# A graph layer on one core: VectorE builds the cells' matrix, its product and the two larger node comparisons in halves

## The chip, the cores and the metric

One core of a Trainium2 chip runs the kernel. The metric is the device time of one execution in microseconds; of several executions the median is taken. Five engines work from queues of their own, each in order: TensorE (PE: matmuls, with the weight loads listed apart as PEld), VectorE (DVE), ScalarE (ACT), GpSimd (POOL, which issues the gathers here) and SyncE (SP, which issues the other transfers). [...]

## The reference

The reference is one layer of a graph network with a residual and a normalization. There are 12,500 nodes with 128 features and 400,000 edges, sorted by their destination. Each edge carries the row of its source through one of two matrices, chosen by its type, and the results are summed per destination:

```python
Xs = X[src]
m_data = Xs @ W_data.T + b_data
m_ctrl = Xs @ W_control.T + b_control
msg = jnp.where((edge_types == 0)[:, None], m_data, m_ctrl)
agg = jax.ops.segment_sum(msg, dst, num_segments=X.shape[0])
out = relu(agg + (X @ W_self.T + b_self))
x = _layernorm(x + out)
```

## The kernel before

The sum over the edges comes first, by type, and the matrices are applied to the sums; so the heavy part is a gather of 400,000 rows and a sum by destination. The edges are 3,125 chunks of 128, in 25 groups of 125 chunks. A group has five windows, and a window five chunks of one kind and twenty of the other.

The five chunks are gathered by GpSimd: an indirect DMA (`fetch`, L828) fetches 128 rows into `msg`. VectorE makes a 0/1 matrix `psel` that says to which destination column each edge goes (`choose` in `gathered`, L850, by `select`, L533), and TensorE multiplies (`add_rows`, L755).

The twenty chunks, 2,560 edges, take another way that needs no gather. There are 107 of these windows, and in the text a window is one of them. The whole node table `x3` stands in SBUF as 98 blocks of 128 rows, and the edges are sorted on the chip by the block of their source into 100 cells of 32 slots. For window `w` this happens in the steps of `give_slots`:

- `block_matrix` (L592): VectorE compares each edge's block number with the 100 cell numbers and writes the 0/1 matrix `O`, 128 x (20 x 100).
- `fours` (L608): sums of chunks of `O` into `prod` (L612, L613). `same_lane` (L597): which chunks of one lane share a block (L602).
- `before` (L615): TensorE counts the edges ahead in the same cell (L622) into PSUM.
- `ranks` (L627): VectorE adds the two counts into `ahead` (L630), multiplies `O` by it into `prod` (L634), and sums `prod` along each row in three steps (L639 twice, L641) into `found`; `rank` is its copy (L643).
- `rank_matrix` (L670): VectorE makes `rm` (L533) and `rv` (L674) from the rank. `put` (L681): TensorE multiplies `O` and `rv` (L686), which puts each edge's lane and code into its cell.
- `spread`, `turn_codes`, `keep_codes`: the cells go through DRAM to all partitions (`pick`) and the codes into `code`.
- In every second window `over` finds edges beyond slot 32 (`key`, `top`, `full`, `over_n`, `bits`), and `spare_slots` gives them 64 spare slots by `om_all` (L558), which TensorE reads at L562.
- `pick_matrix` (L736): VectorE turns `pick` into a 0/1 matrix in place (L741).

Then `picked` (L910) sums the window: TensorE picks the rows of 25 cell quadruples from `x3` (L930, into `got`), ScalarE copies them to `emsg` (L944), VectorE compares each slot's code with the destination columns into `esel` (`choose` in `picked`, L919: 10 quadruples at once, then 9, then 6, each 176 columns wide), and TensorE sums them (L755) into `sums`. VectorE adds `sums` to `acc` and the counts to `cnt` (L817). `sums` has two PSUM banks, the pool of `esel` two buffers, `prod` one.

`finish_batch` multiplies the sums by the weights, and normalizes and writes the rows.

Steps of several windows run beside each other. The program names each step with a place in its window (numbers between 0 and 1), `merged` sorts them, and the framework's scheduler then fixes the order on each engine by dependencies; so the order on VectorE is not quite that of the source. No order is written out by hand, but `issue_after` and `paced` hold some steps behind others.

Of the kernel before, what the change touches and what calls it, by code (L numbers as in the profile page):

```python
# [9 lines left out]
BF = mybir.dt.bfloat16  # L10
# [4 lines left out]
OP = mybir.AluOpType  # L15
# [4 lines left out]
P = 128  # L20
# [9 lines left out]
EC = 20  # L30
# [7 lines left out]
EW = 88  # L38
# [8 lines left out]
NCELL = 4 * NQ  # L47
# [159 lines left out]
def short_path(ctx, tc, const, ident, eps, wT, brow, bad, x, src, dst, etype, ws, bs, out):  # L207
    nc = tc.nc
# [126 lines left out]
    def table(n, base, name):  # L335

        t = keep.tile([P, n], BF, name=name)
        nc.vector.tensor_copy(t, iota([n], [[1, n]], base, 0, f"{name}_i"))
        return t

    cell_cols = [keep.tile([P, NCELL], BF, name=f"cell_col{k}") for k in range(2)]
# [6 lines left out]
    code_col = table(2 * EW, 1, "code_col")  # L348
# [177 lines left out]
    slots, placed = {}, []  # L526
    pairs = len(each_e)

    def select(sel, col, code2):

        rows, n, width = sel.shape
        shape = [rows, n, width // 2, 2]
        nc.vector.tensor_tensor(  # L533
            sel.rearrange("p n (w t) -> p n w t", t=2),
            col[:rows].rearrange("p (o w t) -> p o w t", o=1, t=2).to_broadcast(shape),
            code2.rearrange("p n (o t) -> p n o t", o=1).to_broadcast(shape),
            op=OP.is_equal,
        )
        return sel

    joint = {}

    def spare_slots(w, at):
# [39 lines left out]
    def give_slots(w):  # L583
        g, i = each_e[w]
        blk = codes["e", g][0][:, i]
        blk2, vals2, pk = (t[:, i * CHUNKS + PB:(i + 1) * CHUNKS] for t in codes["e", g][1:])
        s = {}
# [4 lines left out]
        def block_matrix():  # L592
            O = s["held"] = two.tile([P, EC * NCELL], BF, name="O")
            s["O"] = O.rearrange("p (c j) -> p c j", j=NCELL)
            select(s["O"], cell_cols[w % 2], blk2)

        def same_lane():  # L597
            eq = s["prod"][:, :, NCELL:]
# [28 lines left out]
        def ranks():  # L627
            ahead = two.tile([P, NCELL], BF, name="ahead")
            with nc.allow_low_precision(reason="whole numbers; those over 256 need not be exact"):
                nc.vector.tensor_reduce(  # L630
                    ahead, s["ahead"][:, :2 * NCELL].rearrange("p (k j) -> p j k", k=2), AX.X, OP.add
                )
            prod = s["prod"]
            nc.vector.tensor_tensor(  # L634
                prod[:, :, :NCELL], s["O"], ahead.rearrange("p (o j) -> p o j", o=1).to_broadcast([P, EC, NCELL]),
                op=OP.mult,
            )
            for h in ((NCELL + EC) // 2, (NCELL + EC) // 4):
                nc.vector.tensor_add(prod[:, :, :h], prod[:, :, :h], prod[:, :, h:2 * h])  # L639
            found = two.tile([P, EC], FP, name="found")  # L640
            nc.vector.tensor_reduce(found, prod[:, :, :h], AX.X, OP.add)  # L641
            rank = s["rank"] = two.tile([P, EC, 2], BF, name="rank")
            nc.vector.tensor_copy(rank, found.rearrange("p (c o) -> p c o", o=1).to_broadcast([P, EC, 2]))  # L643
# [103 lines left out]
    def sums():  # L747
        return ps2.tile([P, 512], FP, name="sums")

    def cells_of(ps, width, k):  # L750
        return ps[:, k * 2 * width:(k + 1) * 2 * width]

    def add_rows(out, msg, sel, start, stop):
        for j in range(3):
            last = nc.tensor.matmul(  # L755
                out, msg[:, j * D:(j + 1) * D], sel, start=(start and j == 0), stop=stop, skip_group_check=True
            )
        return last
# [54 lines left out]
    def accumulate(at, rows, ps, wide, width):  # L813

        n = rows.shape[1]
        win = rows[:, :, bass.ds(at, width)]
        added.append(nc.vector.tensor_add(win, win, ps[:, :n * wide].rearrange("p (a w) -> p a w", w=wide)[:, :, :width]))  # L817
# [15 lines left out]
    def paced(now, gate):  # L833

        if spare:
            gather = spare.pop()()
        elif to_fetch and due[len(due) - len(to_fetch)] <= now:
            gather = fetch()
        else:
            return  # L840
        tc.add_manual_dep(
            gather.ins, gate.ins.name,
            mybir.DependencyInfo(mybir.DependencyClass.Sync, mybir.DependencyReason.DATA), reason="paced",
        )
# [65 lines left out]
    def picked(w, tiled, ending, before):  # L910

        g, i = each_e[w]
        s = {"sel": {}, "msg": {}}
        bounds = [0, 5, 10, 15, 19, NQ - 1]
        turns = len(bounds) - 1

        def choose(q0, n):  # L919

            sel = select(sp.tile([P, 10, 2 * EW], BF, name="esel")[:, :n], code_col, slots[w]["code"][:, q0:q0 + n])
            for k in range(n):
                s["sel"][q0 + k] = sel[:, k]

        lead = 0 if w % 2 else 2
        half_rows = slice(CAP * lead, CAP * lead + OVF)

        def pick(ps, q, a0=0, a1=4):
            for a in range(a0, a1):
                last = nc.tensor.matmul(  # L930
                    ps[CAP * a:CAP * (a + 1), :], slots[w]["pick"][:, a * NQ + q, :],
                    x3[:, 4 * q + a - a0].rearrange("p j d -> p (j d)"), start=True, stop=True, skip_group_check=True,
                )
            return last

        def rows(q, n, room, half=False):
            ps = psg.tile([P, room, 512], FP, name=f"got{room}")
            msg = two.tile([P, room, 3 * D], BF, name=f"emsg{room}")
            for k in range(n):
                last = pick(ps[:, k, :3 * D], q + k)  # L940
                s["msg"][q + k] = msg[:, k, :]
            if half:
                last = pick(ps[:, n, :3 * D], NQ - 1, lead, lead + 2)
            s["out"] = nc.scalar.copy(msg[:, :n], ps[:, :n, :3 * D])  # L944
            if half:
                nc.scalar.copy(s["msg"][NQ - 1][half_rows, :], ps[half_rows, n, :3 * D])
            return last

        def add(q0, q1):
            done = [  # L950
                add_rows(cells_of(s["ps"], EW, 0), s["msg"].pop(q), s["sel"][q], q == 0, q == NQ - 1)
                for q in range(q0, q1)
            ]
            return done[len(done) // 2 - 1], done[-1]

        def unit(t):

            if t == 3:
                assert not spare
                if "both" in slots[w]:  # L960
                    slots[w]["last"] = two.tile([P, 3 * D], BF, name="last", bufs=1)
                s["msg"][NQ - 1] = slots[w]["last"]
            paced(w + (t + 0.5) / turns, rows(bounds[t], 2, 2))
            if t == 1 and w > 0 and w % 2 == 0:
                spare.append(lambda: spare_rows(w))
            gate = rows(bounds[t] + 2, bounds[t + 1] - bounds[t] - 2, 3, t == 3)
            if t == 0:
                choose(0, 10)
                gates = ending() or [gate]
            if t == 1:  # L970
                choose(10, 9)
            if t == 3:
                choose(19, NQ - 19)
            while counts:
                c = counts.pop(0)
                count(c["ps"], c["sel"])
            if t == 1:
                s["ps"] = sums()
            if t == 1 and before:
                before()  # L980
            if t > 0:
                gates = add(bounds[t - 1], bounds[t])
            paced(w + (t + 1) / turns, gates[0])
            if t == 2:
                paced(w + (t + 1) / turns, gates[-1])
            for u in tiled.get(t, []):
                u()
            if t == 0 and w + 1 < pairs and "own_turn" in slots[w + 1] and w > 0:
                slots[w + 1]["own_turn"]()
            if t == turns - 1 and "both" in slots[w]:  # L990
                with tc.issue_after(s["out"].ins):
                    nc.scalar.copy(slots[w]["last"][:OVF, :], slots[w]["both"][:OVF, :])

        def end():

            early, *more = tiled.get(turns, [lambda: None])
            early()
            gates = add(bounds[turns - 1], NQ)
            for u in more:
                u()  # L1000
            accumulate(place_of(g, 2 * i + 1), acc_rows(g, 0, 2), s["ps"], EW, EW)
            return gates

        return evenly([lambda t=t: unit(t) for t in range(turns)]), end
# [138 lines left out]
    sp = ctx.enter_context(tc.tile_pool(name="sel", bufs=2))  # L1143
# [13 lines left out]
    n = 0  # L1157
# [11 lines left out]
    def ending():  # L1169
        pass  # L1170
# [191 lines left out]
```

## Time and profile before

| what | value |
|---|---|
| median of 3 runs | 1741.98 us (1740.0 to 1743.36) |
| the profiled execution | 1746.84 us, its span 1745.0 us |
| VectorE instructions in the profile | 3677 |
| granted TensorE clock, mean | 0.993 |

The profile is of one execution. A row of the groups gives line, engine, operation, tiles and shapes, the count, then busy us and mean ns of one, then the idle time of the engine just before them and what ended it. A row of the waits says which engine stood, at what, for whom, with the total in us, the count and the longest. The chain of waits is followed back from the last instruction. A mean over forms hides that L533 serves six uses: `O`, `psel`, `rm`, and `esel` in three widths.

### The profile page before, as it was taken

The page shows a single profiled execution, that of the slowest core. Times are in us where ns is not written, and L with a number is a line of the kernel's source. Part 1 is how long each engine was busy: PE and PEld are TensorE (multiplying, and loading weights), DVE is VectorE, ACT ScalarE, POOL GpSimd, SP SyncE. Part 2 cuts the span into 40 slices and gives each one's busy share as a digit, 9 for nine tenths or more (in the row PEclk, how much of TensorE's full clock was granted, in tenths as well). Part 3 has the DMA queues.
Part 4 walks back from the last instruction along what each step waited for, and adds up shares of the span by engine and source line. Part 5 has one row for each costly group of instructions (what it writes and reads, how often), then busy time and mean ns, then how long its engine had stood idle before and what let it go on. Part 6 is the DMA issues. An engine that isn't in the chain of part 4 may idle for free.

```text
span 1745.0 us, 67260 instructions
## 1 busy us (share of the span) xinstructions
PE 1588.9 (91%) x28154; PEld 1238.1 (71%) x28154; DVE 1555.4 (89%) x3677; ACT 1249.5 (72%) x2251; POOL 1266.2 (73%) x1061
## 2 busy tenths in 40 slices
PE   0599999999999999999999999999999999999997
PEld 0377777777777777777777777777777777777776
DVE  7898899999899899899998898999998898998983
ACT  5777777777777777767777777776777676777675
POOL 0277777887778777777777677787777788768772
PEclk9999999999999999999999999999999999999999
DMA  7844454544454444444545444545454545444431
GB/s 202 276 125 145 129 151 129 156 145 145 126 156 127 143 150 139 137 137 131 155 124 160 133 145 129 153 127 155 135 156 127 150 125 146 143 146 126 128 123 59
DMA packets 148966, 248.22 MB, mean 142 GB/s; under 512 B 35937, under 2 KB 115260, under 8 KB 148652
## 3 DMA queue, kind: packets, MB, share of 16 engines
q1 hardware_dynamic: 85994, 134.45, 23.4%
q0 software_dynamic: 50032, 102.98, 22.0%
q10 hardware_dynamic: 12626, 6.40, 1.4%
q8 instruction: 222, 3.64, 0.8%
q14 instruction: 92, 0.75, 0.1%
HBM read 226.24 MB, written 17.50 MB: 140 GB/s over the span
## 4 chain that ended last, share of the span: by engine, by line
PE 43%; DVE 41%; issue 8%; ACT 4%; DMA 3%; DVEq 0%; SPq 0%; POOL 0%; ACTq 0%; POOLq 0%
PE sums L755 19%; PE got L930 14%; DVE esel L533 5%; DVE prod L639 4%; PE side L1049 4%; DVE pick L741 4%; DVE rv L674 3%; DVE found L641 3%; DVE prod L634 3%; DVE prod L612 2%; DVE psel L533 2%; ACT emsg L944 2%; DVE rm L533 2%; PE side L622 2%; DVE O L533 1%
## 5 line engine op out<-in xcount | busy, mean ns | idle before, releaser
L828 POOL DMA_INDIRECT msg<-rows,idx_g x985 | 1194.3, 1213 | 349.0 <-issue 134.4
L944 ACT CAST emsg<-got 128x768 bf16<-128x768 f32 (+1 forms) x1070 | 953.4, 930 | 340.9 <-PE got L930 325.0
L755 PE MATMUL sums<-esel,emsg 128*128 128x176 bf16 x7704 | 693.6, 240 | 2.2 <-DVE acc L817 1.9
L755 PEld LDWEIGHTS <-emsg 128*128 128x128 bf16 x7704 | 566.8, 98 | 111.6 <-issue 104.2
L930 PE MATMUL got<-x,pick 128*32 128x384 bf16 x10486 | 591.9, 331 | 17.8 <-DVE pick L741 10.6
L930 PEld LDWEIGHTS <-pick 128*32 128x32 bf16 x10486 | 242.0, 96 | 139.5 <-DVE pick L741 13.8
L533 DVE TENSOR_TENSOR esel<-code_col,code 128x1760 bf16<-128x1760 bf16 x321 | 293.2, 913 | 20.4 <-PE sums L755 19.0
L755 PE MATMUL sums<-psel,msg 128*128 128x48 bf16 x2955 | 184.3, 184 | 39.8 <-DVE cnt L817 35.8
L755 PEld LDWEIGHTS <-msg 128*128 128x128 bf16 x2955 | 152.6, 97 | 72.9 <-issue 69.4
L639 DVE TENSOR_TENSOR prod<-prod 128x1200 bf16<-128x1200 bf16 x214 | 133.7, 625 | 4.7
L634 DVE TENSOR_TENSOR prod<-O,ahead 128x2000 bf16<-128x2000 bf16 x107 | 128.3, 1199 | 2.7
L533 DVE TENSOR_TENSOR O<-cell_col,blk 128x2000 bf16<-128x2000 bf16 x107 | 127.3, 1189 | 0.5 <-ACT blk L437 0.5
L817 DVE TENSOR_TENSOR acc<-acc,sums 128x176 f32 (+2 forms) x232 | 66.5, 289 | 58.2 <-PE sums L755 49.2
L741 DVE TENSOR_SCALAR pick<-pick,lane_f 128x3200 bf16<-128x3200 bf16 x107 | 112.8, 1054 | 2.8 <-DMA pick<-there 2.8
L905 POOL DMA_INDIRECT both<-rows,idx x54 | 66.5, 1231 | 61.8 <-ACT emsg L944 43.1
L686 PE MATMUL side<-rv,O 128*128 128x64 bf16 x2140 | 84.5, 195 | 21.1 <-DVE rv L674 20.0
L533 DVE TENSOR_TENSOR psel<-near_col,near 128x1200 bf16<-128x1200 bf16 x125 | 96.1, 769 | 0.0
L686 PEld LDWEIGHTS <-O 128*128 128x128 bf16 x2140 | 79.7, 100 | 23.0 <-DVE rv L674 19.8
L674 DVE TENSOR_TENSOR rv<-rm,vals 128x1280 bf16<-128x1280 bf16 x107 | 87.8, 821 | 0.0
L641 DVE TENSOR_REDUCE found<-prod 128x20 f32<-128x600 bf16 x107 | 83.0, 775 | 2.7
L612 DVE TENSOR_TENSOR prod<-O 128x1000 bf16<-128x1000 bf16 x107 | 71.9, 672 | 0.0
L630 DVE TENSOR_REDUCE ahead<-side 128x100 bf16<-128x200 f32 x107 | 38.8, 363 | 32.8 <-PE side L622 29.5
(192 smaller groups left out, 1571.8 us busy)
## 6 DMA issues: line engine op xcount, KB each, us to landing
pick<-there SPq DMA_DIRECT2D x106, 800.0 KB
msg<-rows,idx_g POOLq DMA_INDIRECT x985
acc<-acc_start SPq DMA_DIRECT2D x23, 640.0 KB
rows<-x SPq DMA_DIRECT2D x6, 1344.0 KB
xs<-in_x_dram SPq DMA_DIRECT2D x99, 62.5 KB
out_dram<-h SPq DMA_DIRECT2D x99, 62.5 KB
xt<-in_x_dram ACTq DMA_DIRECT2D x6, 896.0 KB
cnt<-cnt_start SPq DMA_DIRECT2D x22, 160.0 KB
```

What stands on the lines that cost most here:

```text
L533: nc.vector.tensor_tensor(sel.rearrange("p n (w t) -> p n w t", t=2), col[:rows].rearrange("p (o w t) -> p o w t", o=1, t=2).to_broadcast( ...
L612: nc.vector.tensor_add(h[:, :2 * CQ], s["O"][:, :2 * CQ], s["O"][:, 2 * CQ:])
L634: nc.vector.tensor_tensor(prod[:, :, :NCELL], s["O"], ahead.rearrange("p (o j) -> p o j", o=1).to_broadcast([P, EC, NCELL]), op=OP.mult,)
L639: nc.vector.tensor_add(prod[:, :, :h], prod[:, :, :h], prod[:, :, h:2 * h])
L641: nc.vector.tensor_reduce(found, prod[:, :, :h], AX.X, OP.add)
L674: placed[:] = [nc.vector.tensor_tensor(rv.rearrange("p c v (r t) -> p c v r t", t=2), rm.rearrange("p c (o r t) -> p c o r t", o=1, t=2).t ...
L686: nc.tensor.matmul(s["rk"][:m, :2 * CAP], s["held"][:, c * NCELL:c * NCELL + m], s["rv"][:, c].rearrange("p v r -> p (v r)"), start=(c == ...
L741: nc.vector.tensor_scalar(t, t, lane_f, None, op0=OP.is_equal)
L755: last = nc.tensor.matmul(out, msg[:, j * D:(j + 1) * D], sel, start=(start and j == 0), stop=stop, skip_group_check=True)
L828: return nc.gpsimd.indirect_dma_start(out=msg, out_offset=None, in_=rows3[:, :], in_offset=bass.IndirectOffsetOnAxis(ap=codes["p", g][0][: ...
L930: last = nc.tensor.matmul(ps[CAP * a:CAP * (a + 1), :], slots[w]["pick"][:, a * NQ + q, :], x3[:, 4 * q + a - a0].rearrange("p j d -> p (j ...
L944: s["out"] = nc.scalar.copy(msg[:, :n], ps[:, :n, :3 * D])
```

## The change

Three places that issue one VectorE instruction issue two, over the first and the last half of the chunks or quadruples. `halves(n)` gives the two slices; for an odd number the first is longer (9 becomes 5 and 4). The comparison of six quadruples, `psel`, `rm` and everything else stay whole. What is computed is the same, into the same tiles.

```diff
+    def halves(n):
+        return slice(0, n - n // 2), slice(n - n // 2, n)
...
         def block_matrix():
             O = s["held"] = two.tile([P, EC * NCELL], BF, name="O")
             s["O"] = O.rearrange("p (c j) -> p c j", j=NCELL)
-            select(s["O"], cell_cols[w % 2], blk2)
+            for c in halves(EC):
+                select(s["O"][:, c], cell_cols[w % 2], blk2[:, c])
...
             prod = s["prod"]
-            nc.vector.tensor_tensor(
-                prod[:, :, :NCELL], s["O"], ahead.rearrange("p (o j) -> p o j", o=1).to_broadcast([P, EC, NCELL]),
-                op=OP.mult,
-            )
+            for c in halves(EC):
+                nc.vector.tensor_tensor(
+                    prod[:, c, :NCELL], s["O"][:, c],
+                    ahead.rearrange("p (o j) -> p o j", o=1).to_broadcast([P, c.stop - c.start, NCELL]), op=OP.mult,
+                )
...
         def choose(q0, n):
-            sel = select(sp.tile([P, 10, 2 * EW], BF, name="esel")[:, :n], code_col, slots[w]["code"][:, q0:q0 + n])
+            sel = sp.tile([P, 10, 2 * EW], BF, name="esel")[:, :n]
+            for c in halves(n) if n > 6 else [slice(0, n)]:
+                select(sel[:, c], code_col, slots[w]["code"][:, q0 + c.start:q0 + c.stop])
```

## The prediction

> **What bounds the kernel now.** I read the page first: busy times, then the chain of work that ended last.
>
> ```profile
> span 1745.0 us, 67260 instructions
> ...
> PE 1588.9 (91%) x28154; PEld 1238.1 (71%) x28154; DVE 1555.4 (89%) x3677; ACT 1249.5 (72%) x2251; POOL 1266.2 (73%) x1061
> ...
> PE 43%; DVE 41%; issue 8%; ACT 4%; DMA 3%; DVEq 0%; SPq 0%; POOL 0%; ACTq 0%; POOLq 0%
> PE sums L755 19%; PE got L930 14%; DVE esel L533 5%; DVE prod L639 4%; PE side L1049 4%; DVE pick L741 4%; DVE rv L674 3%; DVE found L641 3%; DVE prod L634 3%; DVE prod L612 2%; DVE psel L533 2%; ACT emsg L944 2%; DVE rm L533 2%; PE side L622 2%; DVE O L533 1%
> ```
>
> Two engines carry the end in turn: TensorE with 43% of the chain and VectorE with 41%. The other three are far behind. The busy time of one stretch in the steady part says how much room each of the two has:
>
> ```profile
> core 0: us, PE busy (x) PEld busy (x) DVE busy (x) ACT busy (x) POOL busy (x), PEclk, DMA share, GB/s
> ...
> 800.00:1200.00 400.00, 378.22 (x6752) 295.01 (x6749) 366.62 (x854) 289.08 (x532) 300.44 (x253) 1.00 0.47 140
> ```
>
> TensorE is idle for 22 us in 400 (5%), VectorE for 33 us (8%), and the granted clock is full. Each window (there are 107, so about 16.3 us apiece) leaves 0.9 us of idle TensorE and 1.4 us of idle VectorE. Next, the list of waits tells which of the two waits for the other, and where:
>
> ```profile
> engine line waited for: us in total, times, longest us
> ...
> DVE acc L817 <- PE sums L755: 49.2, 62, 3.4
> ...
> PE sums L755 <- DVE cnt L817: 35.8, 46, 1.9
> ...
> DVE ahead L630 <- PE side L622: 29.5, 51, 3.4
> ...
> DVE esel L533 <- PE sums L755: 19.0, 30, 1.4
> ...
> PE got L930 <- DVE pick L741: 10.6, 15, 2.7
> ...
> PE side L562 <- DVE om_all L558: 9.4, 17, 1.6
> ...
> PE sums L755 <- DVE acc L817: 3.5, 8, 1.7
> ```
>
> Both directions are there. VectorE stands for sums of TensorE (49.2 + 29.5 + 19.0 us), TensorE stands for small VectorE instructions that come late (35.8 + 10.6 + 9.4 + 3.5 us). So the kernel is a coupled pair, each nearly full, and neither more VectorE work nor an earlier small VectorE instruction is free.
>
> **The price of one more VectorE instruction.** The groups by form give the durations of what is cut:
>
> ```profile
> L634 DVE TENSOR_TENSOR prod<-O,ahead 128x2000 bf16<-128x2000 bf16 x107 | 128.3, 1199 | 2.7
> L533 DVE TENSOR_TENSOR O<-cell_col,blk 128x2000 bf16<-128x2000 bf16 x107 | 127.3, 1189 | 0.5 <-ACT blk L437 0.5
> L533 DVE TENSOR_TENSOR esel<-code_col,code 128x1760 bf16<-128x1760 bf16 x107 | 113.4, 1060 | 3.0 <-PE sums L755 2.6
> ...
> L533 DVE TENSOR_TENSOR esel<-code_col,code 128x1584 bf16<-128x1584 bf16 x107 | 104.4, 976 | 0.0
> ...
> L612 DVE TENSOR_TENSOR prod<-O 128x1000 bf16<-128x1000 bf16 x107 | 71.9, 672 | 0.0
> ```
>
> Each of four forms runs 107 times, and the change adds one instruction to each: 4 x 107 = **428** more. By durations, two instructions of 1000 elements take 2 x 672 = 1344 ns against 1189 ns for one of 2000, so 155 ns more. But durations overlap, which the order of time shows by its starts (first column, in us; the second is the duration):
>
> ```profile
> 807.04 0.67 DVE L612 TENSOR_TENSOR prod<-O 128x1000 bf16<-128x1000 bf16 x1
> 807.63 0.37 DVE L602 TENSOR_TENSOR prod<-blk,blk 128x400 bf16<-128x400 bf16 x1
> ...
> 809.30 1.06 DVE L533 TENSOR_TENSOR esel<-code_col,code 128x1760 bf16<-128x1760 bf16 x1
> 810.28 0.17 DVE L651 MAX8 top<-key 128x8 f32<-128x20 f32 x1
> ...
> 814.47 0.97 DVE L533 TENSOR_TENSOR esel<-code_col,code 128x1584 bf16<-128x1584 bf16 x1
> 815.36 1.19 DVE L533 TENSOR_TENSOR O<-cell_col,blk 128x2000 bf16<-128x2000 bf16 x1
> 816.47 0.36 DVE L630 TENSOR_REDUCE ahead<-side 128x100 bf16<-128x200 f32 x1
> ```
>
> An instruction that waits for nothing starts about 0.08 us before the one ahead of it ends. So what the queue feels is start to start: 1.11 us for 2000 elements (815.36 to 816.47), 0.59 us for 1000 (807.04 to 807.63). Two halves take 1.18 us: **0.07 us more**. The comparisons have the same rate: 0.98 us for 1760 and 0.89 us for 1584, that is 0.09 us for 176 elements or 0.51 ns each, which leaves 0.98 - 0.90 = 0.08 us fixed. I take 0.07 us for all four, since the halves wait for nothing of each other (in the built order the second half carries no wait). That is 0.28 us for a window and 428 x 0.07 = **30 us** in all, which is 2% of VectorE's busy time.
>
> [...]
>
> **What of the 30 us shows.** From below: added time shows at least where the halved instructions lie on the chain, as long as the order stays. esel has 5% of 1745 us = 87 us, at 0.83 us a piece (0.98, 0.89 and, for the uncut form of 1056 by the same rate, 0.62) about 105 pieces, of which two forms of three are cut: 70. prod L634 has 3% = 52 us, about 47 pieces of 1.11 us; O has 1% = 17 us, about 15. Together 132 pieces x 0.07 = **9 us**. From above: all 30 us, if VectorE became the only clock. Between: off the chain, VectorE's stalls for TensorE (98 us, 0.9 us a window) take the rest in windows that have such a stall. 62 + 51 + 30 stalls in 107 windows are not spread evenly, so some of the remaining 21 us shows too. I take **15 us**, nearer to the chain's count than to the full sum.
>
> **What the halves could give back.** First, an earlier start for the consumer. TensorE needs only the first columns of esel to begin. But nothing on TensorE waits for esel now; the idle time before everything that writes or reads it ends so:
>
> ```profile
> its engine sat idle before it (us, times) until:
>   PE sums L755: 19.0, 30
>   ACT last L992: 4.8, 1
>   DVE acc L817: 1.9, 2
>   PE side L504: 0.7, 1
>   ACT emsg L944: 0.2, 1
> ```
>
> No row names a VectorE esel, so this gain is nothing. O's readers (the product by ltri behind the fours, and L686) come much later, and the product with ahead goes whole into the add at L639, which waits for the second half. Nothing there either.
>
> Second, **overtaking**. VectorE takes its queue in order, and the order is not that of the source: a scheduler sets it, and with halves it can put a small instruction between them. The built order shows that it does. In 52 of 107 windows something stands between the halves of O, in 80 of 214 cases between those of a comparison, never between those of the product. Against before, about 30 instructions om_all (15 windows) stand ahead of at least half of O; about 20 adds into cnt and 44 into acc stand one half earlier; 16 reductions ahead (L630) stand earlier against O. The rest is all but unchanged: the same instructions on every engine, the order on GpSimd the same in all but two places, and no DMA added or moved past a queue that matters. What an overtaking is worth can be seen in one place:
>
> ```profile
> 465.45 1.07 DVE L533 TENSOR_TENSOR esel<-code_col,code 128x1760 bf16<-128x1760 bf16 x1
> ...
> 466.44 1.19 DVE L533 TENSOR_TENSOR O<-cell_col,blk 128x2000 bf16<-128x2000 bf16 x1
> ...
> 467.55 0.80 DVE L558 TENSOR_SCALAR om_all<-slot_col,side 128x448 bf16<-128x448 bf16 x2
> ...
> 468.41 0.34 PE L562 MATMUL side<-bits_b,om_all 128*128 128x6 bf16 x7 [0.74 <-DVE om_all L558]
> ```
>
> om_all stands behind O (1.11 us), and TensorE idles 0.74 us for it. With om_all behind half of O it would come 0.52 us earlier. The gain at a wait is thus about 0.45 us (half of 1.11, less 0.07 or so for the extra start). How often?
>
> ```profile
> L558 DVE TENSOR_SCALAR om_all<-slot_col,side 128x448 bf16<-128x448 bf16 x107 | 42.9, 439 | 5.5 <-PE side L552 3.8 <-PE sums L755 0.6 <-ACT emsg L944 0.2
> ...
> L817 DVE TENSOR_TENSOR cnt<-cnt,sums 64x120 f32 x120 | 31.6, 263 | 12.4 <-issue 5.6 <-PE sums L755 4.4 <-PE got L930 2.4
> ```
>
> TensorE waits for om_all 17 times in about 53 windows that have it; of the 15 moved ones between 5 (the average share) and 15 (all) hit a wait: 2 to 7 us, I take 4. It waits for 46 of 120 adds into cnt; 38% of 20 moved ones is 8: 8 x 0.45 = 3.5 us, at most 9. The adds into acc hold TensorE 8 times in all: 1 us. The reductions ahead pull the string ahead, L634, L639, found, rank, rm, rv forward; the chain runs through L634 in 47 of 107 windows, so 7 of 16 count, but ahead itself waits for TensorE in half of the windows: 7 x 0.5 x 0.5 = 2 us, at most 8. Sum **10 us**; bounds 0 (every overtaker only waits in front of the queue instead of behind it, as ahead and acc often do) and 25.
>
> **Sum.** 15 - 10 = **+5 us** on the profiled execution of 1746.84 us (span 1745.0, 1.8 us around it). That execution lies 4.9 us above the median of the runs shown, 1741.98 (1740.0 to 1743.36), so I put the difference on the median: **1747.0 us**. Outer bounds: 9 - 25 = -16 (1726) and +30 (1772).
>
> **Rivals.**
> - *The cost shows in full* (VectorE becomes the clock). For it: VectorE has 92% busy in the steady stretch, and the dependent string from ahead to pick holds TensorE at pick. Against it: 98 us of stalls for TensorE. It gives +18 to +30, 1760 to 1772.
> - *The stalls take it all.* For it: three of four cuts lie between pick and the next ahead, where VectorE's stalls for sums and side lie. Against: the 132 pieces on the chain. With 9 to 12 us shown and about 10 given back: 1738.5 to 1745.5, no change that can be told.
> - *Faster: overtaking outweighs the starts.* One mechanism: om_all and cnt come from behind the halves, and TensorE's 35.8 + 9.4 us of waits for them shrink. It decides from the point where more than about 9 / 0.45 = 20 waits are shortened by half an instruction while no more than the chain's 132 pieces pay. With 40 of the 63 waits shortened (40 x 0.45 = 18 us) and 9 us paid it gives -9, 1733. Against: 14 or so waits are hit by the counts above, and most waits for cnt stand behind pick and rv, which are not cut.
> - *Nothing is cut in effect* is no case: the built order has the 428 instructions.
>
> **How the numbers follow.** A measurement of this kernel can tell about 0.2% from no change, that is 3.5 us. Forecast (slower by a little, 1745.5 to 1760): 0.43. Full cost: 0.10. Stalls take it: 0.16. Faster (below 1738.5): 0.31. So slower 0.53, within 0.2% 0.16, faster 0.31. The forecast's own range is 1745.5 to 1760; for 8 in 10 it has to reach well into the faster case and into the lower part of the full cost: 1731 to 1764.
>
> **What would show it.** Right: O, esel and prod in pairs of about 0.67 and 0.6 us, start to start 0.07 us more for a pair; VectorE busy up by 20 to 30 us; the waits of TensorE for om_all down by some us, for cnt a little; the waits of VectorE for sums and side down by more than those of TensorE. Wrong: if pairs cost under 0.03 us more, if TensorE's waits for cnt and om_all fall by over 15 us (faster), or if its waits for pick and cnt rise by over 10 us (full cost). The shape of the scheduler's order over all 107 windows is what I know least: small moves of TensorE's own order could be worth as much as either sum.

## The result and the profile after

The changed kernel takes 1745.7 us (median of 20 runs, 1742.1 to 1750.01), the kernel before 1741.37 us (20 runs, 1737.15 to 1745.67). The ratio is 1.0027, 95% interval 1.0019 to 1.0035: **slower by 0.27%**, 4.7 us by the ratio. The forecast was 5 us on a median of 1741.98 us, that is 1747.0 us; its case, slower by a little, went from 1745.5 to 1760. The measured median lies 0.2 us inside that, right beside the rival in which VectorE's stalls take the starts. The time alone does not tell the two apart; the runs below have to. The two executions that were profiled happen to stand the other way round (1744.97 us after, 1746.84 us before), within the scatter of single runs; so spans of two profiles are compared below only where the difference is much larger. VectorE's busy times are compared: the durations of its 4105 instructions sum to 1859.6 us in the changed kernel and to 1860.8 us with the same halves in the order of before, 0.06% apart.

The page of the changed kernel, its span, busy times and chain:

```profile
span 1743.2 us, 67687 instructions
...
PE 1586.8 (91%) x28154; PEld 1234.6 (71%) x28154; DVE 1576.9 (90%) x4105; ACT 1249.6 (72%) x2251; POOL 1244.5 (71%) x1061
...
DVE 50%; PE 36%; issue 6%; ACT 5%; DMA 2%; DVEq 1%; SPq 0%; ACTq 0%; POOL 0%; POOLq 0%
PE sums L761 16%; PE got L938 12%; DVE esel L533 6%; DVE prod L645 4%; DVE prod L640 4%; DVE pick L747 4%; DVE rv L680 4%; DVE found L647 3%; PE side L1057 3%; DVE prod L617 3%; DVE O L533 2%; DVE psel L533 2%; ACT emsg L952 2%; DVE rm L533 2%; PE side L627 2%
```

VectorE has the 428 instructions more (4105 against 3677) and 21.5 us more of busy time (1576.9 less 1555.4). Its share of the chain goes from 41% to 50%. (L numbers behind the first cut are 5 to 8 higher than those of before. In the runs below with a held order they are up to 49 higher, most of it for the code that holds the order.) The halves by form:

```profile
L533 DVE TENSOR_TENSOR esel<-code_col,code 128x880 bf16<-128x880 bf16 x321 | 188.8, 604 | 4.0 <-PE sums L761 3.6
L533 DVE TENSOR_TENSOR O<-cell_col,blk 128x1000 bf16<-128x1000 bf16 x214 | 138.7, 668 | 0.5 <-ACT blk L437 0.5
L640 DVE TENSOR_TENSOR prod<-O,ahead 128x1000 bf16<-128x1000 bf16 x214 | 135.9, 676 | 2.3
...
L533 DVE TENSOR_TENSOR esel<-code_col,code 128x704 bf16<-128x704 bf16 x107 | 55.4, 518 | 0.0
```

And the waits that answer to those of before:

```profile
DVE acc L823 <- PE sums L761: 40.9, 56, 1.8
PE sums L761 <- DVE cnt L823: 38.7, 57, 1.8
DVE esel L533 <- PE sums L761: 21.5, 24, 1.9
DVE ahead L635 <- PE side L627: 21.0, 40, 2.2
...
PE got L938 <- DVE pick L747: 10.5, 19, 2.6
...
PE side L566 <- DVE om_all L562: 8.4, 14, 1.3
...
PE sums L761 <- DVE acc L823: 4.6, 9, 1.9
```

VectorE stands less for TensorE (40.9 + 21.0 + 21.5 = 83 us where it was 98). TensorE stands for VectorE about as long as before (38.7 + 10.5 + 8.4 + 4.6 = 62 us against 59). The prediction had expected its waits for om_all to fall by some us and those for cnt by a little; against before the first fall by 1.0 us (9.4, then 8.4) and the second rise by 2.9 (35.8, then 38.7). In this comparison nothing of the overtaking can be seen; it takes a kernel that has the starts and not the overtaking.

### The profile page after: what moved, and what is told of

Its sections match the earlier page's. It is cut to its first block, busy times and chain, and to the rows that moved or that the text cites. A ratio compares the mean times of both kernels' runs of the same rounds, so it can differ in the third digit from the quotient of the medians.

```text
span 1743.2 us, 67687 instructions
## 1 busy us (share of the span) xinstructions
PE 1586.8 (91%) x28154; PEld 1234.6 (71%) x28154; DVE 1576.9 (90%) x4105; ACT 1249.6 (72%) x2251; POOL 1244.5 (71%) x1061
## 4 chain that ended last, share of the span: by engine, by line
DVE 50%; PE 36%; issue 6%; ACT 5%; DMA 2%; DVEq 1%; SPq 0%; ACTq 0%; POOL 0%; POOLq 0%
PE sums L761 16%; PE got L938 12%; DVE esel L533 6%; DVE prod L645 4%; DVE prod L640 4%; DVE pick L747 4%; DVE rv L680 4%; DVE found L647 3%; PE side L1057 3%; DVE prod L617 3%; DVE O L533 2%; DVE psel L533 2%; ACT emsg L952 2%; DVE rm L533 2%; PE side L627 2%
## 5 line engine op out<-in xcount | busy, mean ns | idle before, releaser
L834 POOL DMA_INDIRECT msg<-rows,idx_g x985 | 1169.9, 1188 | 361.1 <-issue 121.3
L938 PE MATMUL got<-x,pick 128*32 128x384 bf16 x10486 | 590.6, 331 | 16.1 <-DVE pick L747 10.5
L533 DVE TENSOR_TENSOR esel<-code_col,code 128x880 bf16<-128x880 bf16 (+2 forms) x535 | 313.7, 607 | 23.0 <-PE sums L761 21.5
L761 PE MATMUL sums<-psel,msg 128*128 128x48 bf16 x2955 | 183.2, 184 | 44.5 <-DVE cnt L823 38.7
L533 DVE TENSOR_TENSOR O<-cell_col,blk 128x1000 bf16<-128x1000 bf16 x214 | 138.7, 668 | 0.5 <-ACT blk L437 0.5
L640 DVE TENSOR_TENSOR prod<-O,ahead 128x1000 bf16<-128x1000 bf16 x214 | 135.9, 676 | 2.3
L747 DVE TENSOR_SCALAR pick<-pick,lane_f 128x3200 bf16<-128x3200 bf16 x107 | 113.2, 1057 | 0.8 <-DMA pick<-there 0.8
L823 DVE TENSOR_TENSOR acc<-acc,sums 128x176 f32 (+2 forms) x232 | 66.5, 289 | 48.9 <-PE sums L761 40.9
L627 PEld LDWEIGHTS <-ltri 128*128 128x128 bf16 x1284 | 41.1, 96 | 36.6 <-issue 34.1
```

Source lines behind the costliest of these rows:

```text
L533: nc.vector.tensor_tensor(sel.rearrange("p n (w t) -> p n w t", t=2), col[:rows].rearrange("p (o w t) -> p o w t", o=1, t=2).to_broadcast( ...
L640: nc.vector.tensor_tensor(prod[:, c, :NCELL], s["O"][:, c], ahead.rearrange("p (o j) -> p o j", o=1).to_broadcast([P, c.stop - c.start, NC ...
L747: nc.vector.tensor_scalar(t, t, lane_f, None, op0=OP.is_equal)
L761: last = nc.tensor.matmul(out, msg[:, j * D:(j + 1) * D], sel, start=(start and j == 0), stop=stop, skip_group_check=True)
L834: return nc.gpsimd.indirect_dma_start(out=msg, out_offset=None, in_=rows3[:, :], in_offset=bass.IndirectOffsetOnAxis(ap=codes["p", g][0][: ...
L938: last = nc.tensor.matmul(ps[CAP * a:CAP * (a + 1), :], slots[w]["pick"][:, a * NQ + q, :], x3[:, 4 * q + a - a0].rearrange("p j d -> p (j ...
```

## The experiments

The theory on record: 428 extra starts of 0.07 us show in part (15 us), and small instructions that overtake half of a cut one give back part of that (10 us). Rivals: VectorE's stalls absorb the starts and overtaking is worth nothing; or the starts are free and the new order is what is slower. The two terms come apart if the order is held. Two tools did it: order-only edges (no wait) between each engine's instructions in a given order, and a second half that stands right behind its first ("glued"). The core of it, where `parts[at]` is a whole instruction, or a first half with what is glued to it, and `steps` leads through an engine's instructions in the order that is held:

```diff
+        for d in steps:
+            at += d
+            for i in parts[at]:
+                if before is not None:
+                    tc.add_manual_dep(
+                        i, before.name,
+                        mybir.DependencyInfo(mybir.DependencyClass.NoSync, mybir.DependencyReason.DATA), reason="in_order",
+                    )
+                before = i
```

In the traces, with the pieces of a cut instruction counted as one, VectorE's instructions stand in exactly the order that each run was given. VectorE has 273 semaphore instructions and 2652 instructions with a wait in before, and the same in the two runs with halves and quarters glued in its order: holding the order added no wait. The two orders differ at 768 of 3677 places on VectorE (first halves), 3006 of 27,841 on TensorE, 219 of 2233 on ScalarE and 2 of 1057 on GpSimd. So "all but unchanged", as the prediction had it for the rest of the order, holds for GpSimd alone.

All runs had five rounds beside the kernel before on the same chip: 12 executions for a cut by itself, 4 to 8 for the held orders of the whole change. Microseconds are the ratio's excess times 1741.

| kernel | median us | ratio (95% interval) | us |
|---|---|---|---|
| the change | 1745.70 | 1.0027 (1.0019 to 1.0035) | +4.7 |
| halves glued, order of before | 1754.52 | 1.0078 (1.0063 to 1.0093) | +13.6 |
| quarters glued, order of before | 1790.44 | 1.0286 (1.0269 to 1.0303) | +49.8 |
| whole, order of after, at the second half's place | 1746.49 | 1.0033 (1.0022 to 1.0044) | +5.7 |
| whole, order of after, at the first half's place | 1752.60 | 1.0067 (1.0053 to 1.0082) | +11.7 |
| halves glued, order of after | 1766.44 | 1.0142 (1.0122 to 1.0161) | +24.7 |
| halves glued, VectorE in the order of before, others of after | 1780.86 | 1.0229 (1.0212 to 1.0246) | +39.9 |
| only the cells' matrix cut | 1739.19 | 0.9982 (0.9971 to 0.9994) | -3.1 |
| only the product cut | 1743.70 | 1.0008 (0.9995 to 1.0022) | +1.4 |
| only the comparisons cut | 1745.23 | 1.0021 (1.0011 to 1.0031) | +3.7 |
| cells' matrix cut and glued, order of before | 1745.70 | 1.0027 (1.0014 to 1.0040) | +4.7 |
| cells' matrix whole, order of the run with it cut | 1741.98 | 1.0009 (0.9996 to 1.0022) | +1.6 |
| cells' matrix in quarters | 1742.17 | 0.9999 (0.9987 to 1.0011) | -0.2 |

### The starts alone

> The changed kernel with every engine held in the order of the kernel before; the second half of each cut instruction stands right behind its first half, so nothing overtakes. What is left of the change is the 428 extra starts. My theory (starts that show, less an overtaking that gives back): +9 to +15 us over before, up to 30, VectorE busy up by 20 to 30 us. Rival 'the stalls absorb the starts and the overtaking is worth nothing': +4 us, as the whole change. Rival 'the starts are free, the new order is what is slower': 0, within 2 us.

Measured: +13.6 us (11 to 16). VectorE's busy time is 28.9 us above before, 67.5 ns for each of the 428:

```profile
span 1756.4 us, 67688 instructions
...
PE 1591.8 (91%) x28154; PEld 1240.5 (71%) x28154; DVE 1584.3 (90%) x4105; ACT 1249.0 (71%) x2251; POOL 1238.0 (70%) x1061
```

Both rivals fall: the starts alone cost three times what the whole change costs, so they are neither absorbed nor free. Quarters ask what is left of the cover that VectorE's stalls give:

```diff
-        return slice(0, n - n // 2), slice(n - n // 2, n)
+        ends = [0, *(n - n * k // 4 for k in (3, 2, 1)), n]
+        return [slice(a, b) for a, b in zip(ends, ends[1:])]
```

> As the first run, but in quarters: 1284 extra starts, none overtaken, in the order of before. By 0.07 us apiece 90 us more of VectorE work, 0.84 us for a window, nearly all of VectorE's stalls of 0.9 us. My theory (the cover is used up): 35 to 60 us over before, more than three times the run with halves. Rival 'the stalls absorb the starts': under 20 us.

Measured: +49.8 us, 3.7 times the halves for three times the starts. The page and two of its waits:

```profile
PE 1595.9 (89%) x28154; PEld 1242.6 (69%) x28154; DVE 1641.5 (92%) x4961; ACT 1250.2 (70%) x2251; POOL 1242.2 (69%) x1061
```

```profile
PE sums L802 <- DVE cnt L864: 57.0, 80, 2.2
DVE acc L864 <- PE sums L802: 30.6, 45, 1.5
```

VectorE has 86.1 us more than before for 1284 starts, 67.1 ns each. Of the first 28.9 us 47% showed, of 86.1 us 58%. The waits fit that: VectorE's stalls for TensorE at acc shrink (49.2, then 30.6 us), and TensorE's for the adds into cnt grow (35.8, then 57.0 us).

### The order alone

> The kernel before, every instruction whole, with every engine held in the order of the changed kernel; a whole instruction stands where its second half stood, so the small instructions that overtook half of it now overtake all of it. No extra start. My theory: 5 to 10 us faster than before. Rival 'the stalls absorb the starts': 0, within 2 us. Rival 'the new order is slower': +4 us.

> As the run before, but a whole instruction stands where its first half stood, so the small instructions that came between the halves stand behind all of it, nearly as in the kernel before. My theory: about as before, -2 to +2 us, since the overtaking is gone and no start is added. Rival 'the new order is slower, by TensorE's own order or something else than the halves': +4 us here too.

Measured: +5.7 and +11.7 us. Both of my numbers were wrong, and the first run came near what the rival "the new order is slower" had said (+4). Without any extra start, the order of the changed kernel is slower than that of before, by 12 us where a whole instruction stands in front of what overtook its second half, and by 6 us where all of it is overtaken. So the order is not a thing that is good or bad by itself: the scheduler made it for halves, and the next two runs ask what it needs of them. The place of the small instructions is worth 6 us here (11.7 less 5.7), in the direction that I had expected.

> The changed kernel with every engine held in its own order, but the second half of each cut instruction stands right behind the first, so that the small instructions which stood between the halves stand behind both. If the give-back (9 us between halves in the order of before and the changed kernel) comes from what stands between halves: +10 to +14 us over before, like the halves in the order of before. If it comes from the rest of the new order (whole moves, TensorE's and ScalarE's orders): +4 to +6 us, like the changed kernel.

> Halves glued, VectorE in the order of before, all other engines in the order of the changed kernel. If the give-back lies in VectorE's own order: +12 to +16 us. If it lies in the order of the others: +4 to +6 us.

Measured: +24.7 and +39.9 us, both above both of their expectations. Gluing the halves in the otherwise unchanged order costs 20 us against the changed kernel, so what stands **between** halves is what that order lives on; with nothing between them it is worse than the order of before (13.6). The starts have nearly the same price in both orders: 24.7 less 11.7 is 13.0 us, where in the order of before it was 13.6. In the last run VectorE has one order and the other engines another: it takes 26 us more than the glued halves in the order of before throughout, and 15 us more than those in the order of after throughout. The orders of the engines fit each other, and that is worth at least as much as either term that was forecast (15 and 10 us).

The waits of the glued run, to be held against those of the changed kernel above:

```profile
DVE acc L863 <- PE sums L801: 44.7, 59, 1.8
PE sums L801 <- DVE cnt L863: 44.1, 60, 1.9
DVE ahead L673 <- PE side L665: 29.5, 47, 2.0
DVE esel L569 <- PE sums L801: 25.8, 28, 1.9
PE side L604 <- DVE om_all L600: 14.5, 22, 1.9
```

With the halves apart TensorE waits 6.1 us less for om_all (14.5, then 8.4) and 5.4 us less for cnt (44.1, then 38.7), and VectorE 8.5 us less for ahead.

### Each cut by itself

Two of the three loops were put back to one instruction, and the scheduler was free:

```diff
-            for c in halves(EC):
+            for c in [slice(0, EC)]:
```

> Only the comparison that makes the cells' matrix is cut, 107 extra starts (7 us of VectorE work), the scheduler free as in the change. My theory: starts show +3 us, the overtaking over it gives back 3 to 5 us, so -2 to +1 us against before. Rival 'each cut costs its share': +1 us for a quarter of the extra starts, and nothing between halves matters.

> Only the product with the counts ahead is cut, 107 extra starts, the scheduler free. Nothing ever stands between these halves, so my theory gives the starts alone, and they lie in the string that leads to pick: +3 to +6 us. Rival 'each cut costs its share of the whole': +1 us.

> Only the two larger comparisons of node columns are cut: 214 extra starts, 14 us of VectorE work, the scheduler free. If the three cuts add up: the change's +4 us less -3 (cells' matrix alone) less +1.5 (product alone) leaves +6 us. My theory agrees: starts that show 6 to 7 us (14 us at the share of the halves in the order of before), with little given back. Rival 'the gain of the cells' matrix was chance, each cut costs its share': +2 us.

Measured: -3.1 us (interval -5 to -1), +1.4 us (-1 to +4) and +3.7 us (2 to 5). They add up to +2 us, and the change has +4.7 (3 to 6): the same within the intervals. The comparisons came out between my +6 and the rival's +2. The product is cheaper than I had said and near the rival's +1; its VectorE busy time is 4.3 us up where 107 starts make 7.2. Nothing stands between its halves in any of the 107 windows, so nothing overtook a half of it: the scheduler moved other instructions. **The cells' matrix alone beats both kernels**, by a little more than I had expected; it is the only gain of the study that is clear of zero. Its own starts and its order were then taken apart:

> Only the cells' matrix cut, halves glued, every engine held in the order of before: its 107 starts alone. My theory: +2 to +5 us over before (7 us of VectorE work, of which a half shows), so that the overtaking in the run with the free scheduler gave back 5 to 8. Rival 'O has slack, its starts are free': 0, and then the gain of the free run is the whole worth of the overtaking, 3 us.

> The kernel before, the cells' matrix whole, every engine held in the order of the run with only the cells' matrix cut, the whole where its second half stood. If the place of the small instructions is all that helped, this has the gain without the starts: -3 to -6 us, faster than that run. If the order fits only the durations it was made for: 0 to +4 us.

> Only the cells' matrix cut, in quarters, the scheduler free: 321 extra starts, 21 us of VectorE work. My theory: the starts show 7 to 10 us and the second cut moves the small instructions by a quarter (0.28 us) only, so +1 to +6 us over before. Rival 'finer is better': below -3 us.

Measured: +4.7 us (2 to 7), +1.6 us (-1 to +4), -0.2 us (-2 to +2). So its 107 starts cost 4.7 us, and the free order gives back 7.8. Leaving the starts out and keeping the order does not improve on it. I take the reason to be that a whole matrix in the late place loses what the first half did while the small instruction was not ready yet; no run isolates that. A second cut gains nothing more; I had expected +1 to +6 us for it, and the rival of a finer cut needed less than -3. The waits of TensorE for om_all, glued in the order of before and then free:

```profile
PE side L604 <- DVE om_all L600: 10.9, 20, 1.7
```

```profile
PE side L566 <- DVE om_all L562: 8.0, 14, 1.2
```

That is 2.9 of the 7.8 us. With the matrix whole in the late place TensorE's wait is as short, but now VectorE stands longer at om_all for what it needs from TensorE. First that run, then the free halves:

```profile
PE side L598 <- DVE om_all L594: 7.7, 12, 0.9
...
DVE om_all L594 <- PE side L588: 4.9, 8, 1.3
```

```profile
DVE om_all L562 <- PE side L556: 2.8, 4, 1.3
```

## Why the prediction was right, point by point

- **The price of a start: right.** 0.07 us was taken from starts in the timeline; with the order of before held, each of 428 starts adds 67.5 ns to VectorE's busy time and each of 1284 adds 67.1 ns. In the changed kernel a cut pair in a row looks as forecast:

```profile
811.56 0.67 DVE L533 TENSOR_TENSOR O<-cell_col,blk 128x1000 bf16<-128x1000 bf16 x1
812.15 0.36 DVE L635 TENSOR_REDUCE ahead<-side 128x100 bf16<-128x200 f32 x1
812.42 0.67 DVE L533 TENSOR_TENSOR O<-cell_col,blk 128x1000 bf16<-128x1000 bf16 x1
813.01 1.26 DVE L640 TENSOR_TENSOR prod<-O,ahead 128x1000 bf16<-128x1000 bf16 x2
814.19 0.78 DVE L533 TENSOR_TENSOR psel<-near_col,near 128x1200 bf16<-128x1200 bf16 x1
```

  Each half of O takes 0.59 us from start to start, and the pair of prod 1.18 us (813.01 to 814.19); the reduction ahead stands between the halves of O, as the built order had shown.
- **What of the 30 us shows: right.** 15 us were taken, between 9 and 30; the halves in the order of before show 13.6.
- **The early start of the consumer: not isolated.** Nothing on TensorE waited for esel before, and no row of the idle time before its readers names VectorE's esel after. The comparisons alone cost 3.7 us, so no large gain hides there.
- **The give-back: right in size, half right in cause.** 10 us were taken; 13.6 less 4.7 is 8.9. That is a net of two larger sums which the prediction did not have: the new order with nothing between the halves is 11.1 us slower than the order of before (24.7 less 13.6), and what stands between the halves gives back 20.0. That their difference came near the sum of the prediction's four small terms was partly luck. The prediction's terms were 4 us for om_all, 3.5 for cnt, 1 for acc and 2 for ahead, all of them waits of TensorE or of the string behind ahead. Glued in the order of before the waits that answer to them are these:

```profile
PE sums L801 <- DVE cnt L863: 39.8, 49, 1.8
...
DVE ahead L673 <- PE side L665: 26.6, 49, 2.7
...
PE side L604 <- DVE om_all L600: 11.8, 20, 1.8
...
PE sums L801 <- DVE acc L863: 4.1, 7, 1.8
```

  So from there to the changed kernel om_all gives 3.4 us (11.8, then 8.4), which is the term on record; cnt gives 1.1 instead of 3.5, and acc gives nothing. VectorE stands 5.6 us less at ahead (26.6, then 21.0); what of that reaches the end, no run tells. What the prediction did not have is **VectorE's waits for its own results**. In before, in a place where nothing stands between:

```profile
464.67 0.18 DVE L651 MAX8 top<-key 128x8 f32<-128x20 f32 x1
464.89 0.17 DVE L656 TENSOR_SCALAR full<-top 128x16 f32<-128x16 f32 x1
464.97 0.20 DVE L660 CAST top_i<-top 128x16 int32<-128x16 f32 x1
```

  full needs the result of MAX8 and starts 0.22 us after it, 0.04 after its end. In the changed kernel a half of esel stands between the two:

```profile
805.57 0.18 DVE L657 MAX8 top<-key 128x8 f32<-128x20 f32 x1
805.66 0.60 DVE L533 TENSOR_TENSOR esel<-code_col,code 128x880 bf16<-128x880 bf16 x1
806.18 0.18 DVE L662 TENSOR_SCALAR full<-top 128x16 f32<-128x16 f32 x1
806.27 0.16 DVE L666 CAST top_i<-top 128x16 int32<-128x16 f32 x1
806.35 0.60 DVE L533 TENSOR_TENSOR esel<-code_col,code 128x880 bf16<-128x880 bf16 x1
806.88 0.16 DVE L664 TENSOR_REDUCE over_n<-full 128x2 bf16<-128x16 f32 x1
```

  MAX8 then holds the queue for 0.09 us, and 0.13 us are saved. Counted over the trace by starts and ends, VectorE starts within 0 to 60 ns after the end of the instruction ahead (in before 478 of 507 such starts carry a wait for VectorE's own semaphore) 507 times in before, 512 times with the halves glued in the order of before, and 440 times in the changed kernel. At the same 4105 instructions, whose durations sum to 1860.8 and 1859.6 us, the busy time falls from 1584.3 to 1576.9 us, and the short gaps from 17.3 to 14.9 us: 10 us less of VectorE's queue. How much of these 10 us shows in the time is not shown. At the share at which the starts showed, 47%, it would be about 5 of the 8.9 us, an estimate. And the queue alone does not decide: with the halves glued in the order of after, busy time and short gaps are 1583.9 and 16.2 us, together 1.5 us less than with the halves glued in the order of before, and yet that kernel takes 11 us more. The short gaps also fall without anything between the halves: with only the product cut there are 464. No run takes these waits apart from those of TensorE, so the split stays open.
- **The rivals.** Full cost: 47% of the starts' time showed, so VectorE is not the only clock. The stalls take it all: no, 13.6 us. Faster by overtaking: not as a whole. The cells' matrix by itself is faster (4.7 paid, 7.8 given back), and 2.9 of the 7.8 us are the waits for om_all that this rival names. What the last paragraph of the prediction named as least known, the order of all engines together, turned out at least as large as either term: 15 to 26 us for two orders that do not fit.

## What to carry to other kernels

In this kernel, cutting an instruction of a nearly full engine was paid at each start (67 to 68 ns of busy time). What came back came with an order that puts other instructions between the halves: part of the price for all three cuts together (8.9 of 13.6 us), more than the price for the cells' matrix alone (7.8 against 4.7 us). So cut the one instruction whose wait is seen in the trace behind it (here om_all behind the cells' matrix), not all the long ones. To judge such a change, hold the order of every engine and measure the cut alone: the two terms here were 13.6 and 8.9 us and their difference 4.7. The order that the scheduler made for halves was no gain when it was given to whole instructions (+5.7, +11.7 and +1.6 us).

## What the runs showed of the hardware

With the order of before held, the extra start of a VectorE instruction on 16-bit data cost 67 to 68 ns of busy time, whether it was cut to halves (28.9 us for 428) or quarters (86.1 us for 1284). In before, a VectorE instruction without any wait started 0.08 us before the end of the one ahead (the median of 1299); 478 that waited for VectorE's own semaphore started 0 to 0.06 us after it, 0.04 us in the case shown. The two make 0.12 us, more than the 0.067 us of an extra start, and in the one place of the changed kernel shown above 0.13 us were saved. That an unrelated instruction between two dependent ones pays for its own start is an estimate from these numbers; no run isolates it.
